# Flamingo block with quantized cross-attention and a routed feed-forward: 66 unread transposes on TensorE added to the opening

## The chip, the core and the metric

The kernel runs on one core of one Trainium2 chip. The metric is the device time of one execution in microseconds (us), as the median of several runs. TensorE (PE) does matmuls, transposes and the weight loads that go with them, VectorE (DVE), ScalarE (ACT) and GpSimd (POOL) the rest of the arithmetic, SyncE (SP) issues most DMAs. Each engine works through its own instructions in order and waits on semaphores for the others.

## The reference

The input x is 4 batches of 512 tokens with 512 features. Two residual blocks follow one another.

```python
x = x + tanh(g_xattn) * expert(layernorm(x), fside, ctx)     # per batch b: fside[b] 512x512, ctx[b] 512x256
x = x + tanh(g_ffn) * moe(layernorm(x), ...)

# expert: h = lin(xe, guw); a = silu(h[:, :256]) * h[:, 256:]; return lin(a, dw)
# lin(x, w), per column a smoothing scale, then per row a step size:
s  = sqrt(max(colmax|x|, eps) / max(colmax|w|, eps))
xs, ws = x / s, w * s
xq, wq = round(xs / xscale), round(ws / wscale)              # xscale, wscale: rowmax|.| / 127
out = (xq @ wq.T) * xscale * wscale.T

# moe: softmax over 16 experts, the best 2 per token, at most 256 tokens per expert,
#      gated feed-forward of width 352 per expert, plus a shared one of width 704
```

## The kernel before, in words

Tokens lie on the 128 partitions: a batch is 4 tiles of 128 tokens (TT = 4), the 512 features are 4 blocks of 128 (HC = 4). The kernel has four stages: the opening (batch 0, written out by hand), a planned part (batches 1 to 3 of the first block, with the shared feed-forward filling TensorE), the 16 routed experts, and the sums at the end. Within all of them the instruction order of each engine is fixed when the program is built.

The opening is a list of steps, each given with a time by `opening.at(time, *steps)`; `Program.run` sorts them by that time, then by the order in which they were given, and emits them so. The times are therefore only sort keys: what counts is the place of a step among the others that use the same engine. Nothing is issued "at" 43.0 us; an instruction runs when its engine has come to it and its inputs are there.

The steps of batch 0 that matter here, in order, for the first quantized product (`f0`, from `first(0)`) and the second (`s0`, from `second(0)`):

- `row_rs`, `row_s`: TensorE turns a column of scales into a row on all partitions (`row_broadcast`, L304), ScalarE copies the second one (L475).
- `divide(t)` (L485, VectorE) makes the tile `xn[:, t, :]`; `multiply(t)` (L490) scales the weight tile `wi[:, t, :]` in place, on GpSimd for t = 0 to 2 and on VectorE for t = 3.
- `max_x`, `scale_x`, `steps_x`: row maxima on VectorE, step sizes, integer steps `xq` on ScalarE (L348). `turn_x_tile(t)` transposes each tile (L358) into two PSUM tiles, `take_x` copies them out (L351). The same follows for the weights: `max_w`, `scale_w`, `steps_w`, `turn_w_tile`, `take_w`.
- `product(t)` (L565) is the matmul into `acc`, `scaled` and `times_up` make the gated tile `a3[:, t, :]` (L573, L576, L583).
- `s0` does the same with `a3` and the weights `wc`: `turn_max`, `smooth`, `row_rs`, `row_s`, `divide` (L634, one instruction on all of `a3`), `max_a`, `scale_a`, `steps_a`, `turn_a_tile`, `take_a`, then `max_w` to `take_w`, then `product(t)` (L713 and L719).
- `residual(t)` (L726) adds the result to the tile `X[:, t, :]`, on GpSimd for t = 0 to 2 and on VectorE for t = 3; `stats(t)` (L289, L290, VectorE) writes mean and variance into `mv[:, t, :]`; `norm` is three steps on `mv`: `ve` = variance + eps (L272), a root on ScalarE (L263), and small operations on VectorE (L276 to L283).
- `normal(t)` (L740) makes y, `turn_y(t)` transposes it (L760, four transposes of 128x128) and copies it to `xT` on ScalarE (L351).
- Then come batch 1's absolute maxima (`f1.greater`, L452; `wide1.absolute`, L410; `wide1.greater`, L414), its column maxima (L296), and, between them in a fixed order (`beside`), the first matmuls of the shared feed-forward (L959), which read `xT`.

PSUM is used by three pools: `ps_t` (tag tp, 2 buffers), `ps_c` (tag c, 2) and `ps_mm` (tag mm, 4). `beside_ps` names the last one:

```python
beside_ps = (lambda shape, dt, name: ps_mm.tile(shape, dt, tag="mm", name=name),) * 2
```

From then on `Plan` fixes the order of each engine from costs and needs that are written in the program; that order is not touched by the change.

Of the kernel before, what the change touches and what calls it, by code (L numbers as in the profile page):

```python
# [9 lines left out]
F32 = mybir.dt.float32  # L10
# [10 lines left out]
P = 128  # L21
B, S, H = 4, 512, 512
HC = H // P
# [97 lines left out]
def flamingo_gated_kernel(  # L121
# [17 lines left out]
    vec, act, pe, pool = nc.vector, nc.scalar, nc.tensor, nc.gpsimd  # L139
# [19 lines left out]
    X = const.tile([P, NT, H], F32, tag="X", name="X")  # L159
# [4 lines left out]
    W = [SimpleNamespace() for _ in range(B)]  # L164
# [38 lines left out]
    ident = const.tile([P, P], F32, tag="ident", name="ident")  # L203
# [51 lines left out]
    beside_ps = (lambda shape, dt, name: ps_mm.tile(shape, dt, tag="mm", name=name),) * 2  # L255

    def small(n, name):
        return stat.tile([P, n], F32, tag=name, name=name)
# [971 lines left out]
    opening = Program()  # L1230
    f0, (wide0, narrow0) = first(0), weights(0)
    f1, (wide1, narrow1) = first(1), weights(1, beside_ps)
    s0 = second(0)
    def table(function):
        act.activation(small(1, "warm"), ones[:, :1], function)

    def each(step, *args, ts=range(TT)):
        return [lambda t=t: step(t, *args) for t in ts]

    opening.at(0.0, lambda: table(AF.Sqrt), tables)  # L1240
    opening.at(4.0, *each(f0.stats), every=1.0)
    opening.at(8.4, *f0.norm, every=0.3)
# [5 lines left out]
    opening.at(18.5, f0.smooth[2], f0.row_rs, f0.row_s, gates)  # L1248
    opening.at(19.5, lambda: f1.stats(1), lambda: table(AF.Silu), gate_columns)
    opening.at(20.7, *each(f0.divide), *each(f0.multiply, ts=[0, 1, 2]), f0.max_x, f0.scale_x)  # L1250
    opening.at(26.5, lambda: f0.multiply(3, vec), f0.max_w, f0.scale_w, f0.open_turns)
    opening.at(27.0, *each(f0.steps_x), *each(f0.turn_x_tile))
    opening.at(30.0, lambda: f0.steps_w(3), *each(f0.steps_w, vec, ts=[0, 1, 2]))
# [6 lines left out]
    opening.at(38.7, lambda: f0.times_up(3, vec), lambda: f0.gated_max(2), lambda: f0.gated_max(3))  # L1260
    opening.at(40.0, lambda: table(AF.Sqrt), s0.turn_max, lambda: f1.stats(2), s0.column_max, *s0.smooth)
    opening.at(43.0, s0.row_rs, s0.row_s, lambda: f1.stats(3))
    opening.at(43.7, s0.divide, lambda: s0.multiply(0), lambda: s0.multiply(1), s0.max_a, s0.scale_a)
    opening.at(46.6, lambda: s0.multiply(2, vec), lambda: s0.multiply(3, vec), s0.max_w, s0.scale_w, s0.open_turns)
    opening.at(46.7, *each(s0.steps_a), *each(s0.turn_a_tile), lambda: s0.take_a(act))
# [1 line left out]
    opening.at(51.2, f1.norm[2], *each(f1.absolute), lambda: s0.product(0), lambda: s0.product(1), lambda: s0.residual(0))  # L1267
    opening.at(53.5, lambda: s0.product(2), lambda: s0.residual(1), lambda: s0.stats(0), lambda: s0.product(3))
    opening.at(55.0, lambda: s0.residual(3, vec), lambda: s0.residual(2), lambda: s0.stats(1), lambda: s0.stats(3))
    opening.at(58.0, lambda: s0.stats(2), *s0.norm)  # L1270
    for t in range(TT):
        opening.at(61.0 + 0.5 * t, lambda t=t: s0.normal(t, vec), lambda t=t: s0.turn_y(t))
    sh0 = shared(0)
# [326 lines left out]
    n = plan.add("DVE", 0.0, begin_sums, weights_there, rank=2 * ROUTE)  # L1600
    for i in range(4):
        n = plan.add("DVE", 0.9, lambda i=i: sums[i](), n, rank=2 * ROUTE)
# [13 lines left out]
    n = plan.add("DVE", 0.0, begin_tokens, *joined, n)  # L1616
    for i in range(4):
        n = plan.add("DVE", 0.45, lambda i=i: sums[i](), n)
# [129 lines left out]
```

## Time and profile before

| | |
|---|---|
| time, median of 3 runs | 585.71 us (585.59 to 585.83) |
| time of the profiled execution | 585.57 us |
| span of its profile, first to last instruction | 583.5 us |
| mean granted TensorE clock over the span | 0.977 of full speed |
| instructions in the span | 5816 |
| TensorE matmuls and transposes, busy | 529.3 us (91%), 1760 |
| TensorE weight loads, busy | 275.0 us (47%), 1764 |
| VectorE busy | 405.1 us (69%) |
| ScalarE busy | 228.9 us (39%) |
| GpSimd busy | 138.2 us (24%) |

The span is what the profile covers; the time of the same execution is 2.1 us longer. Times within the profile are us from the start of the span. "PE" is TensorE's matmuls, "PEld" its weight loads, which overlap them. "PEclk" or "clock" is the TensorE clock that was granted, as a share of full speed. In the lines of operations, "out<-in" names what is written and read by the program's names, "xN" is how many, and "[idle before <-releaser]" how long the engine had been idle and which instruction's end let it go on. "L485" is line 485 of the kernel.

### The profile page before, as it was taken

Reading aid. Unit: us, or ns where it says so; the run is one execution under the profiler, and the core shown is the slowest. Engines: PE = TensorE matmul, PEld = TensorE weight load, DVE = VectorE, ACT = ScalarE, POOL = GpSimd, SP = SyncE. Lnnn points to the kernel's source line nnn. Section 1 sums busy time; section 2 is a strip of 40 time slices with the busy share of each in tenths; the row PEclk is TensorE's granted clock in tenths of the full one; section 3 lists DMA queues with packets and bytes.
Section 4 is the critical chain, followed back from the end, with each engine's and each line's share of the span. In section 5 each row is a group of like instructions: output and inputs, shape, how many; then the busy total and the mean of one; then the engine's idle time right before and its main releaser. Section 6 shows DMA issues by size and latency. Waiting matters only on the chain.

```text
span 583.5 us, 5816 instructions
## 1 busy us (share of the span) xinstructions
PE 529.3 (91%) x1760; PEld 275.0 (47%) x1764; DVE 405.1 (69%) x926; ACT 228.9 (39%) x380; POOL 138.2 (24%) x152
## 2 busy tenths in 40 slices
PE   0375499999999999999989999999999999999994
PEld 0232345444444444454455555555555555544441
DVE  3878778998999898987278666666666666304474
ACT  3465366646824272050135434434435343211000
POOL 1212130344143421100310111111212110007770
PEclk9995699999999999999999999999999999999999
DMA  8971012011402365010587999999999995215695
GB/s 295 359 229 38 0 54 92 0 38 54 91 1 54 56 232 155 20 72 1 131 209 223 264 249 269 276 236 276 262 260 274 276 276 173 87 72 160 200 319 187
DMA packets 93774, 95.05 MB, mean 163 GB/s; under 512 B 51488, under 2 KB 69920, under 8 KB 93744
## 3 DMA queue, kind: packets, MB, share of 16 engines
q1 hardware_dynamic: 84016, 69.52, 44.5%
q0 software_dynamic: 5120, 16.78, 9.2%
q10 hardware_dynamic: 4608, 8.39, 3.8%
q8 instruction: 14, 0.23, 0.2%
q14 instruction: 16, 0.13, 0.1%
HBM read 66.36 MB, written 16.78 MB: 142 GB/s over the span
## 4 chain that ended last, share of the span: by engine, by line
PE 79%; DVE 4%; issue 2%; POOL 1%; ACT 0%; DVEq 0%; POOLq 0%
PE b L1138 22%; PE eo L974 14%; PE pu L959 11%; PE pg L959 11%; PE sh L1024 9%; PE pr L998 2%; PE tp_h L1158 2%; PE acc L565 2%; PE sh L1030 1%; PE rowb L304 1%; PE acc L713 1%; DVE amw_w L414 1%; PE tp_am L296 1%; PE tp_x L760 1%; PE tp_q L358 1%
## 5 line engine op out<-in xcount | busy, mean ns | idle before, releaser
L974 PE MATMUL eo<-wd,ehT 128*128 128x512 f32 (+1 forms) x192 | 85.1, 592 | 0.0
L1089 POOL DMA_INDIRECT xg<-xn_dram,slot_token x32 | 34.8, 1088 | 195.7 <-DMA xp<-xg 161.0
L959 PE MATMUL pg<-xT,wsg 128*128 128x512 f32 x160 | 75.7, 603 | 0.0
L959 PE MATMUL pu<-xT,wsu 128*128 128x512 f32 x160 | 74.0, 595 | 0.0
L1024 PE MATMUL sh<-wsd,hT 128*128 128x512 f32 x160 | 73.9, 597 | 0.0
L974 PEld LDWEIGHTS eo<-wd,ehT 128*128 128x128 f32 (+1 forms) x192 | 36.4, 190 | 42.1 <-issue 37.7
L351 ACT COPY xgT<-xp 128x1024 int16<-128x1024 int16 x31 | 39.5, 1339 | 26.4 <-DMA xp<-xg 26.3
L1187 DVE TENSOR_TENSOR p<-p,b 128x352 f32<-128x352 f32 x16 | 8.3, 521 | 58.8 <-PE b L1138 58.8
L1659 POOL DMA_INDIRECT yk<-eo_dram,slot x32 | 33.5, 1048 | 55.7 <-PE pu L959 46.3
L959 PEld LDWEIGHTS pu<-xT,wsu 128*128 128x128 f32 x160 | 29.3, 190 | 31.2 <-issue 31.1
L1024 PEld LDWEIGHTS sh<-wsd,hT 128*128 128x128 f32 x160 | 28.9, 190 | 31.4 <-issue 30.4
L959 PEld LDWEIGHTS pg<-xT,wsg 128*128 128x128 f32 x160 | 29.0, 193 | 30.3 <-issue 29.5
L1138 PE MATMUL b<-T,S 128*128 128x352 f32 x128 | 40.6, 460 | 0.7 <-DVE S L1129 0.7
L1138 PE MATMUL b<-wg,xgT 128*128 128x352 f32 x128 | 40.6, 460 | 0.0
L1138 PE MATMUL b<-wu,S 128*128 128x352 f32 x128 | 40.5, 459 | 0.0
L1149 ACT COPY eo_sb<-eo 128x512 f32<-128x512 f32 x32 | 18.7, 585 | 47.5 <-PE eo L974 43.5
L1138 PEld LDWEIGHTS b<-T,S 128*128 128x128 f32 x128 | 24.2, 190 | 14.5 <-issue 1.2
L1138 PEld LDWEIGHTS b<-wu,S 128*128 128x128 f32 x128 | 24.3, 190 | 13.5
L490 POOL TENSOR_TENSOR wi<-wi,s_row 128x512 f32<-128x512 f32 x15 | 18.6, 1274 | 46.8 <-ACT s_row L475 46.8
L966 DVE TENSOR_TENSOR hT<-g,pu 128x512 f32<-128x512 f32 x20 | 13.6, 682 | 22.6 <-PE pu L959 22.2
L963 ACT ACTIVATE g<-pg 128x512 f32<-128x512 f32 x20 | 11.9, 596 | 41.9 <-PE pg L959 35.6
L1670 DVE SCALAR_TENSOR_TENSOR X<-yk,wk,X 128x512 f32<-128x512 f32 x32 | 23.1, 748 | 7.4 <-DMA yk<-eo_dram,slot 7.1
(219 smaller groups left out, 857.5 us busy)
## 6 DMA issues: line engine op xcount, KB each, us to landing
wg<-in_L_ffn_w_gate_dram SPq DMA_DIRECT2D x16, 704.0 KB, 5.0
wu<-in_L_ffn_w_up_dram SPq DMA_DIRECT2D x16, 704.0 KB, 6.2
wd<-in_L_ffn_w_down_dram SPq DMA_DIRECT2D x16, 512.0 KB, 5.8
eo_dram<-eo_sb ACTq DMA_DIRECT2D x32, 256.0 KB, 4.7
X<-in_x_dram SPq DMA_DIRECT2D x16, 256.0 KB, 8.3
wi<-in_fside_BxS2xS_dram SPq DMA_DIRECT2D x4, 1024.0 KB, 7.1
xn_dram<-yp SPq DMA_DIRECT2D x16, 256.0 KB, 2.0
out_dram<-X SPq DMA_DIRECT2D x16, 256.0 KB, 4.2
```

The source lines that it names most:

```text
L351: return (vec.tensor_copy if on is vec else act.copy)(dst, src)
L490: on.tensor_tensor(w.wi[:, t, :], w.wi[:, t, :], v.s_row, ALU.mult)
L959: pe.matmul(v.ps[name], lhsT=w[:, k, o : o + P], rhs=xT[:, k, :], start=(k == 0), stop=(k == HC - 1))
L963: act.activation(v.g, v.ps["pg"], AF.Silu)
L966: vec.tensor_tensor(dst, v.g, v.ps["pu"], ALU.mult)
L974: pe.matmul(acc, lhsT=hT[:m, c, bass.ts(t, P)], rhs=wd[:m, c, :], start=(c == 0), stop=(c == len(chunks) - 1))
L1024: pe.matmul(accs[t], lhsT=s.hT[:, c, bass.ts(t, P)], rhs=wsd[:, c, :], start=(c == 0), stop=(c == last))
L1089: pool.indirect_dma_start(out=xg.rearrange("p l n -> p (l n)"), out_offset=None, in_=xn_dram, in_offset=bass.IndirectOffsetOnAxis(ap=slot_ ...
L1138: pe.matmul(ps[:, :I], lhsT=lhs[:, k, :], rhs=rhs[:, k, :], start=(first and k == 0), stop=(k == HALF - 1), skip_group_check=not first,)
L1149: act.copy(eo, R[e].acc[h])
L1659: pool.indirect_dma_start(out=yk, out_offset=None, in_=eo_dram, in_offset=bass.IndirectOffsetOnAxis(ap=slot[i % 2][:, tiles[i // 2] : tile ...
L1670: vec.scalar_tensor_tensor(X[:, j, :], yks[added[0]], wk[k][:, j : j + 1], X[:, j, :], ALU.mult, ALU.add)
```

## The change

A function `idle(src, n)` is added. It takes a fresh PSUM tile of the pool `ps_mm` and has TensorE transpose n blocks of `src` into it (4 unless n is given); a `src` of one column is broadcast to a block of 128 x 128. No instruction reads that tile. Calls of `idle` are put at four places of the opening's list: on the tiles `xn` 1 to 3 and `wi` 0 to 2; on `s`, on the four tiles of `a3` (2 blocks each) and on `xs`; on the tiles X 1 to 3 of batch 0; and on the means `mv` of the tiles 1, 3 and 2 and on `ve`. A transpose reads its source, so it can only run when VectorE or GpSimd has written that tile or column. These are 66 transposes, each with its weight load. The step `*s0.norm` is written as its three parts, because some of the calls stand between them. No other step is removed or changes its place.

```diff
--- before.py
+++ after.py
@@ -1237,6 +1237,17 @@
     def each(step, *args, ts=range(TT)):
         return [lambda t=t: step(t, *args) for t in ts]
 
+    def idle(src, n=HC):
+
+
+        tp = beside_ps[0]([P, HC, P], F32, "idle")
+        for k in range(n):
+            block = src[:, bass.ts(k, P)] if src.shape[1] > 1 else src.to_broadcast([P, P])
+            pe.transpose(tp[:, k, :], block, ident)
+
+    def idle_x(t):
+        idle(X[:, t, :])
+
     opening.at(0.0, lambda: table(AF.Sqrt), tables)
     opening.at(4.0, *each(f0.stats), every=1.0)
     opening.at(8.4, *f0.norm, every=0.3)
@@ -1248,6 +1259,7 @@
     opening.at(18.5, f0.smooth[2], f0.row_rs, f0.row_s, gates)
     opening.at(19.5, lambda: f1.stats(1), lambda: table(AF.Silu), gate_columns)
     opening.at(20.7, *each(f0.divide), *each(f0.multiply, ts=[0, 1, 2]), f0.max_x, f0.scale_x)
+    opening.at(20.8, *each(lambda t: idle(f0.xn[:, t, :]), ts=[1, 2, 3]), *each(lambda t: idle(W[0].wi[:, t, :]), ts=[0, 1, 2]))
     opening.at(26.5, lambda: f0.multiply(3, vec), f0.max_w, f0.scale_w, f0.open_turns)
     opening.at(27.0, *each(f0.steps_x), *each(f0.turn_x_tile))
     opening.at(30.0, lambda: f0.steps_w(3), *each(f0.steps_w, vec, ts=[0, 1, 2]))
@@ -1260,6 +1272,8 @@
     opening.at(38.7, lambda: f0.times_up(3, vec), lambda: f0.gated_max(2), lambda: f0.gated_max(3))
     opening.at(40.0, lambda: table(AF.Sqrt), s0.turn_max, lambda: f1.stats(2), s0.column_max, *s0.smooth)
     opening.at(43.0, s0.row_rs, s0.row_s, lambda: f1.stats(3))
+    opening.at(43.0, lambda: idle(s0.s[:, :1]))
+    opening.at(43.8, *each(lambda t: idle(W[0].a3[:, t, :], 2)), lambda: idle(s0.xs[:, :1]))
     opening.at(43.7, s0.divide, lambda: s0.multiply(0), lambda: s0.multiply(1), s0.max_a, s0.scale_a)
     opening.at(46.6, lambda: s0.multiply(2, vec), lambda: s0.multiply(3, vec), s0.max_w, s0.scale_w, s0.open_turns)
     opening.at(46.7, *each(s0.steps_a), *each(s0.turn_a_tile), lambda: s0.take_a(act))
@@ -1267,7 +1281,8 @@
     opening.at(51.2, f1.norm[2], *each(f1.absolute), lambda: s0.product(0), lambda: s0.product(1), lambda: s0.residual(0))
     opening.at(53.5, lambda: s0.product(2), lambda: s0.residual(1), lambda: s0.stats(0), lambda: s0.product(3))
     opening.at(55.0, lambda: s0.residual(3, vec), lambda: s0.residual(2), lambda: s0.stats(1), lambda: s0.stats(3))
-    opening.at(58.0, lambda: s0.stats(2), *s0.norm)
+    opening.at(55.1, *each(idle_x, ts=[1, 2, 3]))
+    opening.at(58.0, lambda: s0.stats(2), s0.norm[0], *each(lambda t: idle(s0.mv[:, t, 0:1]), ts=[1, 3]), lambda: idle(s0.mv[:, 2, 0:1], 3), s0.norm[1], s0.norm[2], lambda: idle(s0.ve[:, :1], 3))
     for t in range(TT):
         opening.at(61.0 + 0.5 * t, lambda t=t: s0.normal(t, vec), lambda t=t: s0.turn_y(t))
     sh0 = shared(0)
```

## The prediction

> **What bounds the kernel now.** I read the page first: the busy tenths by slice, with the clock that TensorE was granted.
>
> ```profile
> PE   0375499999999999999989999999999999999994
> PEclk9995699999999999999999999999999999999999
> ```
>
> From slice 5 (73 us) on TensorE is full; before that it is not, and in slices 3 to 5 its clock was about half. The chain of work that ended last, in order of time, gives the place where TensorE becomes the bound:
>
> ```profile
> 70.92 0.53 ACT ab_w L410
> 71.47 0.70 DVE amw_w L414
> ...
> 73.80 0.68 PE tp_am L296 x4
> ...
> 78.13 1.09 PE rowb L304 x8
> 79.22 1.72 PE pu L959 x4
> ```
>
> Before 78.1 us the chain runs over ScalarE and VectorE with short turns (transposes) of TensorE between them; from 78.1 us to the end it is TensorE work in a fixed order (79% of the span). So whatever brings the row broadcast at 78.13 forward by d should shorten the span by d: the later waits (a stretch of VectorE at 137 to 146 us, others near 226 and 291) hang on work that moves along. Only the opening is then to be computed.
>
> The third view is the table of stretches, cut where the clock changes. Those changes (44.8, 58.4, 61.85, 72.1 us) lie on a grid of 3.41 us: 4, 1 and 3 steps apart. Columns: length, then busy us (and count) of PE, PEld, DVE, ACT, POOL, then the clock granted in it, DMA share, GB/s.
>
> ```profile
> 34.54:37.96 3.42, 3.20 (x11) 1.70 (x11) 1.42 (x3) 2.73 (x6) 0.00 (x0) 1.00 1.04 342
> 41.37:44.78 3.41, 0.44 (x2) 0.20 (x2) 3.13 (x7) 2.84 (x6) 0.73 (x1) 1.00 0.00 0
> 51.61:55.02 3.41, 2.73 (x17) 1.55 (x18) 2.89 (x9) 1.72 (x3) 0.70 (x1) 0.50 0.02 5
> 55.02:58.44 3.42, 3.35 (x10) 1.10 (x9) 2.52 (x8) 2.93 (x5) 1.43 (x2) 0.50 0.51 156
> 58.44:61.85 3.41, 0.23 (x1) 0.00 (x0) 3.34 (x6) 0.68 (x1) 2.65 (x3) 1.00 0.00 0
> 65.26:68.68 3.42, 2.68 (x12) 2.32 (x13) 3.32 (x9) 1.17 (x2) 0.00 (x0) 0.50 0.00 0
> 68.68:72.09 3.41, 3.41 (x12) 2.31 (x11) 1.31 (x2) 2.88 (x6) 0.00 (x0) 0.50 0.00 0
> 573.85:577.26 3.41, 2.14 (x6) 0.68 (x4) 2.07 (x3) 0.00 (x0) 0.00 (x0) 1.00 0.14 53
> ```
>
> The clock of a stretch answers to how busy TensorE was in the one before. A stretch 98% or 100% busy (55.02, 68.68) is followed by full clock; one 7% or 13% busy (58.44, 41.37) by half clock; the one at 573.85, 63% busy, kept the clock. Stretches 78 to 80% busy, nearly all turns (51.61, 65.26), did not raise it. Before 44.8 us the table's 1.00 is only the absence of a record: the durations say half clock until about 38 us (matmuls of L565 0.43 us apart up to 37.8, 0.21 from 39.4 on). So TensorE was cold until 38, from 44.8 to 58.4, and from 61.85 to 72.1.
>
> Last, TensorE's timeline (start, us from first start to last end, then operation):
>
> ```profile
> 54.41 1.06 PE L304 MATMUL rowb<-ident,scw 128*128 128x128 f32 x4
> 55.40 3.27 PE L713 MATMUL acc<-cqT,aqT 128*128 128x512 bf16 x7
> 66.00 3.76 PE L760 MATMUL tp_x<-ident,y 128*128 128x128 f32 x16 [7.33 <-DVE y L740]
> 69.56 1.06 PE L296 MATMUL tp_am<-ident,amx 128*128 128x128 f32 x4
> 78.13 0.65 PE L304 MATMUL rowb<-ident,rs 128*128 128x128 f32 x4 [0.23 <-DVE rs L322]
> 78.61 0.60 PE L304 MATMUL rowb<-ident,s 128*128 128x128 f32 x4
> ```
>
> Cold, a float32 turn follows the one before by 0.22 us (66.00 to 69.56, 16 of them); warm by 0.12 (78.13 to 78.61, four). One alone lasts 421 ns cold, 272 warm.
>
> **What the change adds.** It removes nothing and moves nothing but the closures among which the new turns stand. It adds 66 turns with 66 weight loads: 12 on xn, 12 on wi, 4 on s, 8 on a3, 4 on xs, 12 on X, 11 on mv, 3 on ve. That is 66 x 0.12 = 7.9 us warm, 66 x 0.22 = 14.5 us cold, all on TensorE, all before 66 us. Nothing reads the results. No DMA is added.
>
> What it costs, by group, taken cold, which is the dear end; behind each group stand real turns in TensorE's order:
> - xn and wi. VectorE gives xn tiles 1 to 3 at 24.2, 24.9, 25.6 (22.84 + 0.68 each); GpSimd the wi tiles at 25.6, 26.8, 28.1 (24.36 + 1.24 each). 24 turns from 24.2 at 0.22 end at 29.5; the turns of xq behind them began at 29.52. They are paced by ScalarE, whose last xq tile comes at 31.3, and the copies that wait for them began at 32.79 (ScalarE) and 33.36 (VectorE). Cost 0; without that cover 0.2.
> - s, a3, xs. From 48.0 (end of the row broadcasts) 4 turns to 48.9; a3 is there at 48.91, so 8 to 50.7; xs at 50.4, so 4 to 51.6. The turns of aq began at 51.18: 0.4 late. But their last tile comes at 52.33, and six short turns at 0.11 are done by then. Cost 0; without that cover 0.4.
> - X, mv, ve. X tiles come at about 59.8, 61.1 (GpSimd) and 61.6 (VectorE); mv at 62.5, 63.2, 64.0, ve at 64.25. The last three turns end at 64.9 cold; the turns of y behind them began at 66.00. Cost 0, slack 1.1.
> The PSUM buffers are the four of the matmul pool; between 35.6 and 69 us nothing else lives in them. GpSimd's multiply takes 1.24 us beside a nearly idle TensorE (24.36) and 1.25 beside a full one (79.92), so reads of the same SBUF cost nothing that shows. Fetching 132 more instructions is not shown separately; between 0 and 0.3 us, I take 0, since it lies in waits.
>
> What it gives, if turns count as work for the clock:
> - The stretch 24.30 to 27.72, empty before, is full of turns; the clock rises at 27.7 instead of 38. The 16 short turns of wq took 0.11 each, ended near 34.5, and the copies waited for them: VectorE 0.4 us, ScalarE 0.8. Warm they end 0.25 after the last wq tile (33.44), so VectorE starts 0.4 and ScalarE 0.7 earlier. Both lead to h at 38.62, but VectorE has an unexplained 0.53 us pause just before it, which may swallow this. 0 to 0.7, I take 0.5.
> - 41.37 to 44.78 gets no new turns, so the clock falls at 44.8 as now. 48.2 to 51.6 becomes 90% full; the clock rises at 51.6 instead of 58.4. Then the copy of cqT (waited 0.4 on turns) starts 0.25 earlier. The products at L713 come 0.21 apart, not 0.43: VectorE's first o waited 0.38 and its third 0.34 for them. From the third o on VectorE is gapless to the end of the statistics (64.0). Together 0.4 to 0.9, I take 0.7, which is the two waits on the products; GpSimd's root (54.32 to 55.37) holds back the rest.
> - Four warm turns keep TensorE busy for 0.63 us (3 x 0.12 + 0.27), three for 0.51. With those on X, 58.44 to 61.85 has 0.23 + 3 x 0.63 = 2.1 us (62%), and with those on mv and ve 61.85 to 65.26 has 2 x 0.63 + 2 x 0.51 = 2.3 us (67%). If that holds the clock, the turns of y run warm. The four copies to xT on ScalarE waited for them 3.5 us in total and ended at 70.39. Warm, the first starts 0.5 earlier (a group of four takes 0.63 against 1.1), and then ScalarE's own 0.59 sets the pace instead of 0.22 x 4 = 0.9. So 66.65 + 4 x 0.6 = 69.1: 1.3 earlier. ab_w, the head of the chain, follows directly. 0.9 to 1.4.
> Sum 0.5 + 0.7 + 1.3 = 2.5 us, from 1.3 to 3.0. Matmuls at 70.44 that become warm add nothing: TensorE then waits longer for VectorE at 73.8.
>
> [...] Either turns count, with a threshold between 80 and 94% (the stretch from 34.54), or matmuls for half a stretch suffice. No row shows a stretch full of turns alone, nor two thirds full of them while warm. I take the row, at about two to one, because holding needs less than raising: 63% held, where 80% did not raise.
>
> **Rivals.** The profiled execution took 585.57 us (span 583.5, 2.1 around it); the median is 585.71, 0.14 more.
> - Main case: turns raise and hold the clock. 585.57 - 2.5 = 583.1, at the median 583.2; own range 582.7 to 584.4. Chance 0.48.
> - Half: they do only one of the two, since 90% is under the threshold for raising, or 62% of turns under that for holding. Then 0.5 + 0.7 = 1.2 or 1.3 alone: 584.5. For it: both shares lie in the gaps that the rows leave open. Chance 0.18.
> - The change doesn't do what it says: turns do not count. 585.7, within 0.4, since they lie in waits. Chance 0.24.
> - Slower: VectorE's multiply of wi tile 3 (28.63, L490) would have to wait until the turns on wi have been read, if accesses are ordered by whole tile and not by block. They end at 29.5 cold plus 0.4 for the last: 1.25 us on VectorE, whose maxima, steps and turns of wi all follow. 587.0. It decides as soon as that order is kept by tile. Against it: X is one tile, and VectorE wrote block 3 at 60.62 while GpSimd wrote block 2 until 61.1. Chance 0.10.
>
> **How the numbers follow.** A measurement can tell about 0.2%, 1.2 us, from no change, so faster means below 584.5. Main case 0.48 and half of the second 0.09: faster 0.57. The other half 0.09 and the third 0.24: same 0.33. Slower 0.10. The range from 582.5 to 586.0 leaves out the slower case and a sliver below.
>
> **What would show it.** Clock 1.00 from 51.6 to the end without the drop at 61.85; the turns of y 0.12 apart; ScalarE's last xT copy near 67.9; the row broadcast of 78.13 near 75.6, and the same distance from there to the end. I am wrong if the turns run and the clock's stretches are as before, or if VectorE's multiply at 28.63 shows a wait on TensorE.

## The result, and the profile after

| | before | changed |
|---|---|---|
| time, median (of 20 runs each, same chip) | 585.42 us (584.46 to 586.06) | 584.21 us (582.71 to 585.60) |
| ratio | | 0.9981 (95%: 0.9973 to 0.9989) |
| profiled execution: time, span | 585.57, 583.5 us | 584.21, 582.1 us |
| mean granted clock | 0.977 | 0.984 |

The changed kernel is faster by 0.19%, 1.1 us (0.6 to 1.6). The forecast was 583.2 us in a range from 582.5 to 586.0: right in sign and inside the range, but the gain is less than half of the 2.5 us that were worked out. 0.19% also lies just within the 0.2% that the forecast called "same", although its interval excludes no change.

The busy tenths and the clock of the changed kernel, from its page:

```profile
PE   0666699999999999999989999999999999999994
PEclk9986899999999999999999999999999999999999
```

TensorE is now busy throughout the opening, and the clock is higher in slices 3 to 5, but not full. Why not is seen in the table of stretches, cut on this execution's grid (length, then busy us and count of PE, PEld, DVE, ACT, POOL, the clock granted in it, DMA share, GB/s):

```profile
23.62:27.03 3.41, 3.30 (x18) 2.87 (x17) 3.38 (x5) 2.82 (x5) 2.18 (x2) 1.00 1.12 329
27.03:30.45 3.42, 3.42 (x19) 3.08 (x17) 3.17 (x7) 2.13 (x5) 1.55 (x2) 1.00 1.06 323
30.45:33.86 3.41, 1.99 (x23) 1.16 (x22) 3.31 (x6) 2.55 (x5) 0.00 (x0) 1.00 1.05 357
...
47.51:50.93 3.42, 3.32 (x16) 2.92 (x16) 3.24 (x7) 0.37 (x1) 1.42 (x2) 0.50 0.00 0
50.93:54.34 3.41, 2.29 (x19) 1.15 (x18) 3.20 (x10) 2.72 (x5) 0.00 (x0) 1.00 0.00 0
...
57.75:61.17 3.42, 1.79 (x8) 0.66 (x7) 3.35 (x6) 1.73 (x3) 3.42 (x3) 1.00 0.00 0
61.17:64.58 3.41, 3.08 (x15) 3.09 (x16) 3.27 (x8) 0.00 (x0) 0.27 (x1) 0.50 0.00 0
64.58:67.99 3.41, 2.44 (x20) 1.93 (x19) 3.00 (x11) 1.15 (x3) 0.00 (x0) 1.00 0.00 0
```

Unread turns alone do raise the clock: 61.17, filled at half clock with turns on X and mv and nothing else, is followed by full clock. So are 47.51 (the turns on s and a3 behind real ones) and 27.03 (the last turns on xn, those on wi and the first of xq; the record begins at 30.4, and the turns before that follow each other at 0.21 us, so 1.00 is once more an absent record). But three raised stretches lose the clock at once: 30.45, 50.93 and 57.75, busy for 58%, 67% and 52%, are followed by half clock.

The timeline of TensorE in the last wait and after it (the turns of y are those of L760):

```profile
60.27 0.66 PE L1246 MATMUL idle<-ident,X 128*128 128x128 f32 x4 [1.22 <-POOL X L726]
61.49 1.97 PE L1246 MATMUL idle<-ident,X 128*128 128x128 f32 x8 [0.57 <-POOL X L726]
63.26 2.02 PE L1246 MATMUL idle<-ident,mv 128*128 128x128 f32 x11
65.11 0.49 PE L1246 MATMUL idle<-ident,ve 128*128 128x128 f32 x3
66.35 1.11 PE L760 MATMUL tp_x<-ident,y 128*128 128x128 f32 x8 [0.75 <-DVE y L740]
67.69 1.15 PE L760 MATMUL tp_x<-ident,y 128*128 128x128 f32 x8 [0.22 <-DVE y L740]
77.19 0.65 PE L304 MATMUL rowb<-ident,rs 128*128 128x128 f32 x4 [0.23 <-DVE rs L322]
```

The turns on X 2, X 3 and most on mv ran cold (at half clock, 0.21 us apart), because the clock fell at 61.17; they were done before y came, and raised the clock at 64.58, just ahead of the turns of y. Those, 0.11 us apart where they were 0.21 before, end at 68.8 instead of 69.8, and the row broadcast starts at 77.19 instead of 78.13.

**How to compare two openings.** Loading varies from one execution to the next: ScalarE's wait for the DMA of wi ends at 10.25 us in the profile before and at 10.73 after, and VectorE's first reciprocal (L276) starts at 11.53 and 12.01, ahead of any added turn; over all 14 profiles it lies between 10.4 and 12.1. So openings are compared from there on. In the table "to ve" is the way from that reciprocal to ve of the last normalization (L272), "to rows" from ve to the row broadcast (L304), behind which TensorE is the bound.

| kernel (runs) | to ve | to rows | sum | ratio of times |
|---|---|---|---|---|
| before | 52.55 | 14.05 | 66.60 | |
| changed, 66 turns | 52.42 | 12.76 | 65.18 | 0.9981 (0.9973 to 0.9989) |
| the same, second run | 52.37 | 12.76 | 65.13 | 0.9970 (0.9960 to 0.9981) |
| only X, mv, ve (26), two runs | 52.57, 52.65 | 12.76, 12.76 | 65.33, 65.41 | 0.9982 (0.9962 to 1.0003), 0.9994 (0.9987 to 1.0000) |
| only the other 40, two runs | 51.48, 51.82 | 14.05, 13.76 | 65.53, 65.58 | 0.9999 (0.9979 to 1.0019), 1.0006 (0.9996 to 1.0016) |
| 45 in the last wait | 52.59 | 12.76 | 65.35 | 1.0005 (0.9982 to 1.0029) |
| 26 in a burst, two runs | 52.60, 52.69 | 14.05, 14.05 | 66.65, 66.73 | 1.0073 (1.0044 to 1.0102), 1.0016 (1.0010 to 1.0023) |
| 135 turns | 51.34 | 12.75 | 64.09 | 0.9966 (0.9954 to 0.9979) |
| 135 turns, later add | 50.67 | 12.75 | 63.43 | 0.9942 (0.9928 to 0.9956) |
| later add, no turns | 52.22 | 13.77 | 65.99 | 0.9991 (0.9983 to 1.0000) |
| 66 turns, later add | 51.43 | 12.76 | 64.19 | 0.9969 (0.9959 to 0.9980) |

The opening of the changed kernel is 66.60 - 65.18 = 1.42 us shorter, and 1.47 in the second run. Two kernels without any turn on X, mv or ve (the later add, and the second run of the 40 turns) reach the row broadcast 0.28 us sooner after ve than the kernel before: there the clock rose 5.0 us after ve, and 6.2 or more in the other four without such turns or with them in a burst. So differences of about 0.3 us behind ve can come from the place of the grid alone.

### The profile page after: what moved, and what is told of

Same layout as the page of the kernel before. It is cut to its first block, busy times and chain, and to the rows that moved or that the text cites. A ratio compares the mean times of both kernels' runs of the same rounds, so it can differ in the third digit from the quotient of the medians.

```text
span 582.1 us, 5953 instructions
## 1 busy us (share of the span) xinstructions
PE 537.7 (92%) x1826; PEld 284.1 (49%) x1830; DVE 405.4 (70%) x926; ACT 228.4 (39%) x380; POOL 138.8 (24%) x152
## 4 chain that ended last, share of the span: by engine, by line
PE 83%; DVE 4%; issue 1%; ACT 0%; DVEq 0%
PE b L1138 22%; PE eo L974 14%; PE pu L959 12%; PE pg L959 11%; PE sh L1024 11%; PE pr L998 2%; PE tp_h L1158 2%; PE acc L565 2%; PE sh L1030 1%; PE rowb L304 1%; PE acc L713 1%; DVE amw_w L414 1%; PE tp_x L760 1%; PE tp_am L296 1%; PE tp_q L358 1%; PE logit L773 1%
## 5 line engine op out<-in xcount | busy, mean ns | idle before, releaser
L959 PE MATMUL pg<-xT,wsg 128*128 128x512 f32 x160 | 74.8, 597 | 0.0
L959 PE MATMUL pu<-xT,wsu 128*128 128x512 f32 x160 | 74.0, 595 | 0.0
L1187 DVE TENSOR_TENSOR p<-p,b 128x352 f32<-128x352 f32 x16 | 8.3, 521 | 59.9 <-PE b L1138 59.9
L959 PEld LDWEIGHTS pu<-xT,wsu 128*128 128x128 f32 x160 | 29.3, 190 | 31.2 <-issue 31.1
L1024 PEld LDWEIGHTS sh<-wsd,hT 128*128 128x128 f32 x160 | 28.9, 190 | 31.4 <-issue 30.4
L959 PEld LDWEIGHTS pg<-xT,wsg 128*128 128x128 f32 x160 | 28.7, 190 | 29.6 <-issue 29.0
L1149 ACT COPY eo_sb<-eo 128x512 f32<-128x512 f32 x32 | 18.7, 585 | 49.3 <-PE eo L974 43.3
L1138 PEld LDWEIGHTS b<-wg,xgT 128*128 128x128 f32 x128 | 23.1, 190 | 10.9 <-issue 0.8
```

Source lines behind the costliest of these rows:

```text
L959: pe.matmul(v.ps[name], lhsT=w[:, k, o : o + P], rhs=xT[:, k, :], start=(k == 0), stop=(k == HC - 1))
L1024: pe.matmul(accs[t], lhsT=s.hT[:, c, bass.ts(t, P)], rhs=wsd[:, c, :], start=(c == 0), stop=(c == last))
L1138: pe.matmul(ps[:, :I], lhsT=lhs[:, k, :], rhs=rhs[:, k, :], start=(first and k == 0), stop=(k == HALF - 1), skip_group_check=not first,)
L1149: act.copy(eo, R[e].acc[h])
```

## The experiments

The first four ran on a chip where the end took longer (from the last add of L1187 to the end 89 to 92 us, against 81.2 in the other ten profiles; the kernel before took 595 us there and scattered by 14). In three of these profiles VectorE stands still for 11 to 13 us among the adds of the gathered results. So the ratios say little; the openings can be read all the same. Three of them were therefore timed again on another chip.

**One group of turns at a time.** Only the last 26 turns, on X, mv and ve (the lines below taken out), and only the other 40:

```diff
-    opening.at(20.8, *each(lambda t: idle(f0.xn[:, t, :]), ts=[1, 2, 3]), ...)
-    opening.at(43.0, lambda: idle(s0.s[:, :1]))
-    opening.at(43.8, *each(lambda t: idle(W[0].a3[:, t, :], 2)), lambda: idle(s0.xs[:, :1]))
```

> Keeps only the 26 unread turns on X, mv and ve; those on xn, wi, s, a3 and xs are taken out. Last-wait theory (all of the gain comes from y's turns running warm, because the turns just before them raise or hold the clock): ratio about 0.998, as with all 66; in the profile the turns of y 0.12 us apart, the last copy to xT about 3.6 us after ve against 6.3 before, and the row broadcast after batch 1's maxima (78.13 before) about 1.2 earlier, counted from ve. Early theory (the gain comes from the 40 turns on xn, wi, s, a3 and xs, which start the work earlier): ratio 1.000, and ve no earlier than in the kernel before.

> Keeps only the 40 unread turns on xn, wi, s, a3 and xs; those on X, mv and ve are taken out. Last-wait theory: ratio 1.000 (0.9995 to 1.0005): the clock may rise at about 30 and 51 us and fall again, TensorE is idle from 58.7 to 66 and y's turns run cold, 0.22 us apart. Early theory: ratio about 0.998.

In the opening the last 26 turns give 1.29 us between ve and the row broadcast, and nothing before it: the last-wait theory holds for that part. But the early theory is not wrong. The other 40 gave 1.07 us before ve. Of this, 0.63 us was there already at h (L573, the first product): the clock rose at 28.8 us and held to 45.9, where the changed kernel lost it at 33.9 and had h only 0.20 us earlier. The rest came behind, where the clock stayed up for two stretches:

```profile
49.29:52.70 3.41, 3.19 (x19) 2.62 (x17) 3.17 (x8) 1.88 (x5) 0.33 (x1) 0.50 0.00 0
52.70:56.12 3.42, 2.48 (x15) 1.28 (x17) 2.81 (x12) 1.74 (x3) 1.05 (x1) 1.00 0.26 70
56.12:59.53 3.41, 1.18 (x4) 0.29 (x3) 3.32 (x7) 2.71 (x4) 2.90 (x3) 1.00 0.24 86
```

The grid lay 1.9 us later against the work here than in the changed kernel's profile, so that the stretch after the rise (52.70) held the turns of cq, the row broadcast and the first products, and kept the clock for them. In the second run the grid lay 0.8 us later: h was again 0.63 us earlier, but the second rise (51.1) was lost at 54.5, and the sum was 0.73. So the same 40 turns give 0.73 and 1.07 us at these two places of the grid, and 0.13 and 0.18 at that of the changed kernel.

Both were timed again:

> The 26 turns on X, mv and ve alone, on another chip: the first one was bound at its end by the gathers of the results, and its times scattered by 10 us and more. Last-wait theory, as its profile showed (1.3 us from ve to the row broadcast): ratio 0.9978 (0.997 to 0.9985). If the 40 other turns have a share in the time at most phases: 0.999.

> The 40 turns on xn, wi, s, a3 and xs alone, on another chip. They gave 1.1 us in the one profile in which the clock they raised lasted to 45.9 and from 52.7 to 59.5, and 0.1 to 0.2 in the two profiles of all 66. If phases of the first kind are rare: ratio 0.9995 (0.999 to 1.000). If they are common: 0.998.

Measured: 0.9994 (0.9987 to 1.0000) and 1.0006 (0.9996 to 1.0016), in openings 1.19 and 1.02 us shorter. The first misses its range, and in both the time shows less than the opening: some 0.8 and 1.4 us of the shorter opening do not reach the end in the median. In the two profiled executions they do (spans of 582.5 and 582.4 us against 583.5 in the profile before), so what was lost in the others is not seen in any trace.

**More turns in the last wait.**

```diff
-    opening.at(55.1, *each(idle_x, ts=[1, 2, 3]))
+    opening.at(55.1, lambda: idle(X[:, 0, :], 8), lambda: idle(X[:, 1, :], 8), lambda: idle(X[:, 2, :], 5), lambda: idle(X[:, 3, :], 5))
```

> As the first, but 45 turns in the last wait instead of 26: 8, 8, 5, 5 on X 0 to 3 (X 0 is new), 5, 5, 3 on mv, 6 on ve. Hold theory (the clock falls in the wait because a 3.41 us stretch is filled too little, so that only some phases of the grid give y's turns the full clock): clock 1.00 from about 58 us to the end in the profile, ratio 0.9965 to 0.9975, less spread between runs than 2.9 us. Backlog theory (more turns, when they start cold at 0.22 us each, are still in the queue when y comes): y's first turn more than 0.6 us after y is ready, ratio 0.999 or worse.

The clock stayed at 1.00 from 59.55 to the end of the stage, and nothing was pushed back. But "to rows" is 12.76, as with 26 turns: y's turns had been warm there too. The time (1.0005, 0.9982 to 1.0029) misses the expected 0.9965 to 0.9975, but was inconclusive on that chip.

**One burst without release.**

```diff
-    opening.at(55.1, *each(idle_x, ts=[1, 2, 3]))
+    opening.at(55.1, *[lambda: idle(ident, 1)] * 12)
...
```

> The same 26 turns at the same places in TensorE's order, but all read the identity matrix, so nothing releases them piece by piece: they run in one burst directly after the last product. If it matters that each is released by a result in the wait: the burst ends by 62 (warm) or 64.5 (cold), the clock falls one stretch later, y's turns are cold in most runs, ratio 0.9990 to 1.0000. If only their number counts: ratio 0.998, y's turns 0.12 apart.

```profile
58.14 3.00 PE L1246 MATMUL idle<-ident 128*128 128x128 f32 x26
65.75 3.76 PE L760 MATMUL tp_x<-ident,y 128*128 128x128 f32 x16 [4.61 <-DVE y L740]
```

All 26 ran by 61.1, the clock fell at 63.2, and y's turns were cold: 14.05, as before. What helps is that the results release the turns through the wait: with the 26 released so it is 12.76. The ratio of 1.0073 on this chip lies far outside what was expected. Again on the other chip:

> The 26 turns on the identity matrix, in one burst after the last product, on another chip. If they are as good as absent, as the opening of its profile said (the row broadcast 14.05 us after ve, as before): ratio 0.9995 to 1.0005. If the excess on the first chip (1.007) belongs to the kernel and not to its end there: 1.003 or more.

1.0016 (1.0010 to 1.0023), between the two expectations: 0.9 us slower, though the opening is as before within 0.13 us. In its profile the excess lies in the middle stage (see below).

**Enough turns in every stretch.** Turns were added where the waits were thin: on xn 0 between the turns of xq and wq; 19 on a3 while its tiles come; 10 on f1's mv and on s2; more on s, a3, xs; 8 on wc; and the last wait as above.

```diff
+    opening.at(30.2, lambda: idle(f0.xn[:, 0, :], 4))
+    opening.at(39.0, *each(lambda t: idle(W[0].a3[:, t, :], 4), ts=[0, 1]), lambda: idle(W[0].a3[:, 2, :], 8), lambda: idle(W[0].a3[:, 3, :], 3))
+    opening.at(40.0, lambda: idle(f1.mv[:, 2, 0:1], 4), lambda: idle(s0.s2[:, :1], 6))
...
```

> 135 unread turns in place of 66, laid so that from 30 to 66 us every 3.41 us stretch has TensorE's array in work for half of its length or more, counting 0.12 us for a float32 turn, 0.055 for a 16-bit turn and 0.215 for a matmul of L713 or L565 (warm). Hold theory (below some 45% of array work the clock falls; the 66 turns are too thin in most waits, hence half of the forecast gain): clock 1.00 from about 30 us to the end; from the first small operation after the first statistics (11.53 before) to ve of the last one 1.3 us less than before, from there to the row broadcast (78.13 before) 1.3 us less; ratio 0.9955 where the end of the kernel is not bound by the gathers. Backlog theory (more turns push real ones back): real turns start more than 0.5 us after their inputs, ratio 0.998 or worse.

The clock from its page, and the stretches of the last wait:

```profile
PEclk9999999999999999999999999999999999999998
```

```profile
54.93:58.35 3.42, 2.66 (x14) 1.32 (x13) 3.29 (x9) 2.94 (x4) 2.24 (x2) 1.00 0.40 136
58.35:61.76 3.41, 2.99 (x24) 2.34 (x23) 3.34 (x5) 0.00 (x0) 1.50 (x2) 1.00 0.02 5
61.76:65.17 3.41, 2.65 (x22) 1.98 (x19) 2.90 (x13) 0.20 (x1) 0.00 (x0) 1.00 0.00 0
```

Full clock from 27.6 us on, and the opening is 2.51 us shorter, 1.21 of it before ve and 1.30 behind it. The time follows with 0.9966 (0.9955 was expected), 2.0 us.

**VectorE's add behind GpSimd.** In the changed kernel VectorE was 0.54 us earlier with its third o, and yet ve came only 0.13 earlier. The two engines' adds to X, of the changed kernel:

```profile
60.61 1.38 DVE L726 TENSOR_TENSOR X<-X,o 128x512 f32<-128x512 f32 x1
57.72 3.73 POOL L726 TENSOR_TENSOR X<-X,o 128x512 f32<-128x512 f32 x3 [1.99 <-DVE o L719]
```

VectorE's add lasts 1.38 us and ends at 61.99, 0.54 after GpSimd's third add (61.45). Before, it lasted 1.01 (60.62 to 61.63), again 0.54 after GpSimd's (61.09). In all eleven profiles in which the add keeps its place it ends 0.54 or 0.55 us after GpSimd's. The experiment moves it behind the statistics of tile 1, with the 135 turns, alone, and with the 66:

```diff
-    opening.at(55.0, lambda: s0.residual(3, vec), lambda: s0.residual(2), lambda: s0.stats(1), lambda: s0.stats(3))
+    opening.at(55.0, lambda: s0.residual(2), lambda: s0.stats(1), lambda: s0.residual(3, vec), lambda: s0.stats(3))
```

> As the one before, and VectorE's add of X tile 3 stands behind the statistics of tile 1 and not ahead of them. Port theory (the add waits for GpSimd, which is still adding tile 2: it lasted 1.01 and 1.38 us and ended 0.54 after GpSimd's third add both times): here it lasts about 0.7, ve comes another 0.3 to 0.6 us earlier, ratio 0.995. Otherwise the add lasts as long at its new place and ve comes no earlier.

> The kernel before with nothing but that move of VectorE's add; no unread turns. Port theory: the add lasts about 0.7 us instead of 1.01, ve 0.3 earlier, ratio 0.9995. Otherwise 1.01 and ratio 1.000.

> The changed kernel with VectorE's add of X tile 3 behind the statistics of tile 1. Port theory: the add lasts 0.7 instead of 1.36 to 1.38 us, and the gains add up: the 1.4 of the turns and some 0.6 of the add; ratio 0.9965. If the later add only moves the wait to the next statistics: ratio as without it, 0.9975.

Alone, the add became

```profile
61.78 0.66 DVE L726 TENSOR_TENSOR X<-X,o 128x512 f32<-128x512 f32 x1
57.83 3.73 POOL L726 TENSOR_TENSOR X<-X,o 128x512 f32<-128x512 f32 x3 [2.00 <-DVE o L719]
```

0.66 us, after GpSimd's end at 61.56, and ve came 0.33 earlier. With the 135 turns it lasts 0.72 and ve comes 0.67 earlier than without the move; with the 66 turns ve is 0.94 to 0.99 earlier than in the two runs without it, of which about 0.3 comes from another place of the grid (the first o was already that much earlier). What is shown is that the add, begun beside GpSimd's (0.2 to 0.9 us ahead of its end), ends 0.54 or 0.55 us after that one is over, that it lasts 0.66 us behind it, and that the place in the order decides between the two. What holds it up beside GpSimd's, the port of the expectations or something else, is not shown by any run. The 135 turns with the later add are the fastest version: 581.89 us against 585.58, ratio 0.9942 (0.9928 to 0.9956).

**The changed kernel once more.**

> The changed kernel once more, for a second look at where the clock's grid falls and for a time beside the others on the same chip. Phase theory (the grid of 3.41 us has no fixed place against the kernel's start): the clock changes at other times than 30.4, 33.9, 37.3 and so on, other real operations are warm, and ve and the row broadcast move by some tenths; ratio 0.998. Otherwise the clock changes at the same times within 0.5 us.

The clock changed at 29.7, 33.1, 36.5, 43.3, 50.2, 53.6, 57.0, 60.4 and 63.8: all about 0.75 us earlier than in the first profile. But the first reciprocal came 0.83 earlier too, so against the work the grid lay almost as before, and the opening was the same to 0.05. Against the work it does move: counted from the first reciprocal, the first rise of kernels with the same work up to there lies at 26.4 (before), 24.5 and 25.5 (26 turns, two runs) and 26.5 us (later add).

## Why the forecast was right in sign and too large

**Turns count for the clock: right.** Stretches that hold turns and nothing else (27.03 and 61.17 in the changed kernel) are followed by full clock, from 30.45 and 64.58 on.

**Holding the clock: wrong, and this is the step that failed.** The forecast read holding from the column of busy time, where 63% had held, and took two thirds as enough. But the column does not sort the stretches. One of the burst kernel's is busy for 50% with eight matmuls and keeps the clock (full until 46.1):

```profile
39.32:42.73 3.41, 1.69 (x8) 0.58 (x6) 3.21 (x8) 2.34 (x7) 2.15 (x3) 1.00 0.01 3
```

The one at 50.93 above, 67% busy with short turns, loses it; the one at 23.62, 97% busy at half clock, does not raise it. Busy time is the wrong measure for short turns: at full clock a 16-bit turn is shown for 0.22 us, but in a row they follow each other by 0.056. Counted by such spacings, called array time here (0.11 us a float32 turn, 0.056 a 16-bit one, 0.215 a matmul of L565 and L713, 0.43 one of L959; about twice that at half clock: 0.21, 0.107 and 0.43 for the first three), the stretches of the 14 profiles fall into order much better. As estimates, since single records are missing: at half clock none with less than 0.75 of its length in array time raised the clock and all from 0.85 on did; at full clock all from 0.45 on kept it and all below 0.30 lost it; in between there were both. The one at 39.32 has 0.45; the three that lost the clock in the changed kernel have between 0.33 and 0.38; that at 23.62 has 0.79, if the four 16 x 16 turns of L230 in it are counted by their size, at an eighth of the others; by their spacing of 0.107 us it would have 0.89 and be the one exception. The same count for turns and matmuls fits both. Hence, by the forecast's steps:
- xn and wi, 0.5 expected: the clock rose at 30.4, not 27.7 (the stretch from 23.62, with 0.79 of it in array time, did not raise it; the one from 27.03, full of turns, did), and fell at 33.9, before the last turns of wq. h at L573 came 0.2 us earlier. With the clock held (135 turns, and both runs of the 40) it was 0.63 to 0.64.
- s, a3, xs, 0.7 expected: the clock rose at 50.9 as forecast and fell at 54.3, before the products. The way to ve is 0.13 shorter in all, less than the 0.2 won before. With the clock held, the first o came 1.2 us earlier than before and ve 1.2. The third o's wait of 0.34, which the sum counted, brought nothing in either, since GpSimd's adds set the end; the statement that VectorE was gapless and so bound by itself overlooked that about a third of its add of 1.01 us goes beyond the 0.66 that it takes behind GpSimd's adds.
- y's turns, 1.3 expected: 1.29 or 1.30 measured, in each of the eight profiles with the turns on X, mv and ve released through the wait. The size was right, but by another way than forecast in the changed kernel: in both its profiles, and in one of the 26 turns, the clock was not held but fell and was raised anew ahead of y. In the other five it stayed up from 59.6 us or earlier.
Sum 0.2 - 0.1 + 1.3 = 1.4 against 2.5; the time shows 1.1 of it. That the size of 2.5 was right for a held clock is shown by the 135 turns: 2.51.

**Costs at nothing: right.** The 66 turns stand in waits, and y's turns began within 0.1 us of y. VectorE's multiply of wi tile 3 began without a wait on TensorE. What fetching 132 more instructions takes, set at 0 in the forecast, no run shows by itself. The rival in which turns do not count, and the slower one, fell with that.

**From the row broadcast on: only partly right.** The forecast passed a shorter opening on to the end in full. The stage of the experts, from the first to the last add of L1187, took 208.6 to 208.7 us in all 14 profiles. But the middle stage, from the row broadcast to its begin, takes 215.1 to 216.9 us. Counted from the row broadcast, VectorE's distance from the kernel before changes in jumps, the largest near 152 and 195 us, where it waits for transposes by DMA, and near 229 us, where it waits for GpSimd's scaled wc (L637). VectorE's cast of the third batch's weights, with 26 turns released and in the burst:

```profile
195.21 0.69 DVE L379 CAST wqT<-wqT 128x2048 bf16<-128x2048 int16 x1 [0.64 <-DMA wqT<-wq]
```

```profile
197.49 1.18 DVE L379 CAST wqT<-wqT 128x2048 bf16<-128x2048 int16 x1 [1.29 <-DMA wqT<-wq]
```

Up to there both run alike, counted from the row broadcast (to 0.02 us), and the second of the two transposes is issued at 114.02 and 114.03 us. It lands at 117.94 and 118.58, and in the kernel before at 117.12. The cast lasts 1.18 us in the burst and 1.32 before. At its end both runs of the burst lie 1.3 us behind the kernel before; in all, their middle stage is 0.8 and 1.4 us longer. The delay of this cast comes again in the second run of the same kernel, on another chip: 0.7 us in both runs of the 26 turns, 0.9 and 1.1 with the 40, 1.4 in both of the burst. So it belongs to the kernel, though the order of VectorE's instructions in the middle stage is the same in all. What decides when these transposes land was not found. The 26 turns alone and the 40 alone gain less time (0.35 us and nothing) than their openings (1.2 and 1.0), while all 66 (1.1 and 1.8 against 1.4) and the 135 (2.0 against 2.5) come near theirs. Why is open as well. These transposes cannot be the whole of it: in the two profiles of the 26 turns the middle stage is at most 0.1 us longer than before.

## What to carry to other kernels

In these profiles TensorE's clock was kept, lost and regained stretch by stretch on the 3.41 us grid, and it was array time, not the busy column, that sorted the stretches. As estimates from them: one with 0.45 of it or more always kept the clock and one with less than 0.30 never did; once lost, the clock came back always behind 0.85 and never behind less than 0.75. Spread such work over the waits by letting results release it: here, a burst of the same size did nothing (14.05 us from ve to the row broadcast, as without it, against 12.76). And before a gain is passed on through a stage, look for the operation there that lasts longer beside another engine's than behind it (here 1.01 and 1.38 us against 0.66).

## What had not been expected of the hardware

The grid of the clock had no fixed place against the kernel's work: from one execution to the next the first rise of comparable openings moved by 2 us (24.5 to 26.5 us after the first reciprocal). VectorE's add, begun beside GpSimd's, ended 0.54 to 0.55 us after it in eleven profiles, while statistics, which read X alone, took 0.68 or 0.69 us beside it and 0.66 to 0.68 behind it. And a DMA transpose of the middle stage, issued 114.0 us behind the row broadcast each time, took 3.1 us to landing in the kernel before, 3.9 with the 26 turns and 4.5 in the burst.
